# Two selective-scan layers on one core: the instruction order taken from a timeline of engines and queues

## The chip, the cores and the metric

The kernel runs on one core of a Trainium2 chip. Times are device microseconds of one execution. The kernel before takes 29334.67 us, the median of three runs (29313.72 to 29365.72).

A core has five engines that run side by side, each with a queue of its own that is worked off strictly in order: PE (matrix products, written to PSUM), DVE (vector work), ACT (activation functions and copies), POOL (elementwise work in SBUF) and SP (here used to issue DMAs; ACT issues some too). An instruction that depends on another engine waits on a semaphore, and everything queued behind it on its engine waits with it.

## The reference

Sixteen images of 48 x 48 positions with 96 channels go through two layers. Each layer is a state-space block (a "selective scan" in four directions) and a small feed-forward net with values rounded to 8-bit floats. In outline, with the shapes of one image (L = 48 x 48 = 2304):

```python
xc, z = split(layernorm(x) @ in_proj_w.T)            # 192 channels each
xc = silu(depthwise_conv3x3(xc) + conv_b)
xs = [rows, columns, rows reversed, columns reversed]   # 4 directions of xc
dts, B, C = split(x_proj_w @ xs)                     # 6, 16 and 16 rows per direction
delta = softplus(dt_proj_w @ dts + dt_proj_b)
for t in range(L):                                   # 192 channels x 16 states x 4 directions
    h = exp(delta[t] * A) * h + (delta[t] * xs[t]) * B[t]
    y[t] = sum_over_states(h * C[t])
y = merge of the four directions + Ds * xs
# layer 0: y * silu(z) -> out_proj, plus a branch: 1x1, depthwise 3x3 (384 channels), 1x1, gate
# layer 1: layernorm(y) * silu(z) -> out_proj
x = x + that
x = x + feed_forward(layernorm(x))                   # fp8 products, fp16 sums
```

## The kernel before, in words

**The scan.** For each image and layer the recurrence is done by `scan` (line 448). A tile has 128 partitions: 32 channels times 4 states. Along the free axis lie 768 of the 2304 positions. One *step* is one such tile; a layer of one image takes 288 of them (two pairs of directions, three blocks of positions `c`, three blocks of channels `j`, four groups of channels `i`, four groups of states `g`), and the whole kernel 9216. A step does this:

```python
nc.scalar.activation(a, d[:, 0, :], AF.Exp, scale=rates[...])                 # line 484, ACT, into PSUM
nc.gpsimd.tensor_tensor(b, d[:, 1, :], bc[:, 0, :], ALU.mult)                 # line 486, POOL
nc.vector.tensor_tensor_scan(way(h), way(a), way(b), start, ALU.mult, ALU.add)  # line 518, DVE
(nc.vector if here else nc.gpsimd).tensor_tensor(hc, h, cc, ALU.mult)         # line 520
nc.scalar.copy(carry[:, at : at + 1], h[:, last : last + 1])                  # line 522, ACT
nc.tensor.matmul(py[:, q, :SUB], lhsT=self.fold[:, i, :], rhs=hc[...])         # line 524, PE, two of them
```

The scan writes over `a` in three steps of four, and DVE then does the product with C; in the fourth it writes to a tile `h` of its own, and POOL does that product. `a` has two PSUM buffers, `b` four, `hc` four, the loaded `d` (delta and delta times u, line 466) four and `bc` (B and C, line 475) six. The sum over states is left to PE, which adds up 16 steps in the PSUM tile `py`; ACT copies that to `yt` (line 533) and stores it. The first product into `py` (line 504) adds the skip term or the result of the first pair of directions.

**The other work.** Everything that is not a scan runs in Python generators beside the scan of another image or layer: `first` and part of `middle` prepare a scan (`before`, line 346: norm, transposes L300, in-projection L358/L361, convolution L333, SiLU L372, reordered copies L375/L378, the products for B, C and dt L412/L416, `dl` with Softplus L430/L431/L435, `du` on POOL L442, stored by SP L443); `middle` and `final` finish one (`merge` L545 to L553, `gate` L568 to L577, `branch` L593 to L632 with three more convolutions, `centred` L677 to L700, `add_out` L644, `feed_forward` L705 to L742). A 3 x 3 convolution is nine matmuls for each 384 positions (one *chunk*, L333), accumulated in a PSUM tile `pst`. All products of the other work share two buffers of `pst` (line 268), which ACT or DVE empties.

**What sets the order.** `together` (line 781) interleaves one scan of 288 steps, here called a *phase*, with one or two of these generators: after each step it takes as many pieces of the other work as the estimates in the `yield` statements and the totals in `WORK` (line 777) allot to it, up to 94% of the phase (`AHEAD`). There are 32 phases. Two of four hold `final` and `first`, two hold `middle`, which has more convolutions.

This Python order is not yet the order on the engines. The kernel is written in a layer that records instructions and the tiles they touch, and orders them on leaving its context (line 890). Its scheduler plays the program on a model of the machine: an instruction is issued to its engine's queue when, in that model, its inputs are there and its buffers are free, and among those that are ready the one recorded first goes first. The result is one fixed list per engine, with semaphore waits added afterwards. How long things take in the model therefore decides which instruction stands before which on the same engine.

## Time and profile before

| | us |
|---|---|
| median of three runs | 29334.67 |
| the profiled execution | 29326.56 |
| its span, first to last instruction | 29324.8 |
| PE busy | 24033.6 |
| PE weight loads | 12726.8 |
| DVE busy | 23488.3 |
| POOL busy | 23241.6 |
| ACT busy | 14074.7 |
| mean granted PE clock | 0.898 |

The page names a group of instructions by line, engine, operation and tiles (output <- inputs), its shape and count; then its busy time and the mean of one in ns; then the idle time of the engine just before these instructions, and which instruction ended most of it. A fp32 matmul shows as two passes (x36864 for 18432 instructions). In the list of waits a row reads: the engine and instruction that waited, the one that it waited for, microseconds in total, number of waits, the longest. In the timeline a row reads: start, duration, engine, line, operation, tiles, count, and in brackets the idle time before it and what ended it. A row of the stretches gives for each engine the busy time and the number of instructions in that window.

By phase, the profile is very regular: phases with `middle` take about 937 us, the others about 882 us; the first scan starts at 214.6 us, and the last ends about 167 us before the end.

### The profile page before, as it was taken

Reading aid. Unit: us, or ns where it says so; the run is one execution under the profiler, and the core shown is the slowest. Engines: PE = TensorE matmul, PEld = TensorE weight load, DVE = VectorE, ACT = ScalarE, POOL = GpSimd, SP = SyncE. Lnnn points to the kernel's source line nnn. Section 1 sums busy time; section 2 is a strip of 40 time slices with the busy share of each in tenths; the row PEclk is TensorE's granted clock in tenths of the full one; section 3 lists DMA queues with packets and bytes.
Section 4 is the critical chain, followed back from the end, with each engine's and each line's share of the span. In section 5 each row is a group of like instructions: output and inputs, shape, how many; then the busy total and the mean of one; then the engine's idle time right before and its main releaser. Section 6 shows DMA issues by size and latency. Waiting matters only on the chain. (4 is left out here: it accounts for less than half of the span.)

```text
span 29324.8 us, 227106 instructions
## 1 busy us (share of the span) xinstructions
PE 24033.6 (82%) x68224; PEld 12726.8 (43%) x68224; DVE 23488.3 (80%) x18372; ACT 14074.7 (48%) x22093; POOL 23241.6 (79%) x13238
## 2 busy tenths in 40 slices
PE   7888878888788887888788887888778888788886
PEld 3444444444444444444444444444444444344443
DVE  6877888778887788877888778887788877888777
ACT  4454444544445454444444444444444444444443
POOL 6877788778887788877888778787787877877777
PEclk8988899989999899998999989999898998989988
DMA  4444444444444444444444444444444344443443
GB/s 155 153 156 152 146 148 155 154 151 149 148 152 154 154 152 148 148 156 149 159 143 151 151 149 160 144 148 153 150 164 145 141 154 150 162 148 143 150 156 109
DMA packets 1062581, 4406.37 MB, mean 150 GB/s; under 512 B 211936, under 2 KB 211936, under 8 KB 1030368
## 3 DMA queue, kind: packets, MB, share of 16 engines
q1 hardware_dynamic: 869792, 3757.78, 36.2%
q10 hardware_dynamic: 191552, 634.06, 5.5%
q8 instruction: 536, 8.78, 0.1%
q14 instruction: 701, 5.74, 0.1%
HBM read 3500.22 MB, written 891.22 MB: 150 GB/s over the span
## 5 line engine op out<-in xcount | busy, mean ns | idle before, releaser
L486 POOL TENSOR_TENSOR b<-d,bc 128x768 f32<-128x768 f32 x9216 | 16584.7, 1819 | 4084.2 <-DVE a L518 2783.7
L524 PE MATMUL py<-hc,fold_sb 128*128 128x384 f32 x36864 | 14564.0, 540 | 3265.9 <-DVE hc L520 1991.2
L524 PEld LDWEIGHTS py<-hc,fold_sb 128*128 128x128 f32 x36864 | 7359.8, 208 | 9807.3 <-DVE hc L520 3050.8
L484 ACT ACTIVATE a<-d,l_a 128x768 f32<-128x768 f32 x9216 | 8304.2, 906 | 5248.7 <-DVE h L518 2817.0
L518 DVE TENSOR_TENSOR_SCAN a<-a,carry,b 128x768 f32<-128x768 f32 x4608 | 8252.7, 1813 | 2037.9 <-ACT a L484 1438.6
L520 DVE TENSOR_TENSOR hc<-a,bc 128x768 f32<-128x768 f32 x6912 | 6427.8, 947 | 1034.1 <-PE py L524 873.5
L520 POOL TENSOR_TENSOR hc<-h,bc 128x768 f32<-128x768 f32 x2304 | 4187.6, 1818 | 1511.8 <-DVE h L518 1115.4
L518 DVE TENSOR_TENSOR_SCAN a<-a,b 128x768 f32<-128x768 f32 x2304 | 4002.9, 1755 | 1091.6 <-ACT a L484 612.1
L522 ACT COPY carry<-a 128x1 f32<-128x1 f32 x4608 | 725.2, 158 | 5229.7 <-DVE hc L520 5210.7
L518 DVE TENSOR_TENSOR_SCAN h<-a,carry,b 128x768 f32<-128x768 f32 x1536 | 2766.9, 1801 | 484.0 <-ACT a L484 354.4
L333 PE MATMUL pst<-e,dg 128*128 128x384 f32 x5184 | 1730.3, 486 | 0.0
L430 PE MATMUL pst<-dts,wpack_sb 24*128 24x384 f32 x2304 | 1200.8, 636 | 513.9 <-ACT dl L431 434.2
L518 DVE TENSOR_TENSOR_SCAN h<-a,b 128x768 f32<-128x768 f32 x768 | 1337.2, 1741 | 303.9 <-POOL b L486 236.0
L333 PEld LDWEIGHTS pst<-e,dg 128*128 128x128 f32 x5184 | 977.2, 189 | 705.5 <-PE py L524 25.5
L333 PE MATMUL pst<-wxa,dg 128*128 128x384 f32 x3456 | 1173.3, 492 | 24.9 <-DMA dg<-taps_l0a 20.0
L442 POOL TENSOR_TENSOR du<-dl,u 128x768 f32<-128x768 f32 x576 | 1033.6, 1809 | 201.2 <-DMA dd<-du 100.4
L333 PE MATMUL pst<-wxb,dg 128*128 128x384 f32 x3456 | 1169.7, 489 | 5.6 <-issue 5.6
L431 ACT ACTIVATE dl<-pst,wpack_sb 128x384 f32<-128x384 f32 x1152 | 644.0, 577 | 1072.5 <-PE pst L430 581.4
L430 PEld LDWEIGHTS pst<-dts,wpack_sb 24*128 24x128 f32 x2304 | 446.7, 223 | 1206.6 <-ACT dl L431 661.4
L504 PE MATMUL py<-first,ident 128*128 128x384 f32 x1152 | 570.7, 629 | 484.5 <-ACT yt L533 479.6
L412 PE MATMUL pst<-u,wpack_sb 128*24 128x384 f32 (+1 forms) x2304 | 831.7, 492 | 65.2 <-ACT u L395 23.0
L333 PEld LDWEIGHTS pst<-wxa,dg 128*128 128x128 f32 x3456 | 661.5, 192 | 509.4 <-issue 44.6
(143 smaller groups left out, 15283.5 us busy)
## 6 DMA issues: line engine op xcount, KB each, us to landing
d<-dd SPq DMA_DIRECT2D x2304, 768.0 KB, 4.6
bc<-bc SPq DMA_DIRECT2D x1536, 768.0 KB, 6.0
dd<-dl ACTq DMA_DIRECT2D x192, 1152.0 KB, 4.7
dd<-du SPq DMA_DIRECT2D x576, 384.0 KB, 2.5
y<-yt ACTq DMA_DIRECT2D x576, 384.0 KB, 3.1
u<-u ACTq DMA_DIRECT2D x96, 1152.0 KB, 5.1
first<-u SPq DMA_DIRECT2D x288, 384.0 KB, 3.3
first<-y SPq DMA_DIRECT2D x288, 384.0 KB, 3.1
```

What stands on the lines that cost most here:

```text
L333: nc.tensor.matmul(img(o[:, :SUB]), lhsT=dg[:, k, :], rhs=img(p, PW)[:, PQ * q + i : PQ * q + i + PQ, j : j + HW], start=(k == 0), stop=(k ...
L412: nc.tensor.matmul(o[:m, :SUB], lhsT=w[:, j, :], rhs=u[j][:, cs], start=(j == 0), stop=(j == 2))
L430: nc.tensor.matmul(o[:, :SUB], lhsT=dtw[:, col, :], rhs=dts[:, cs], start=True, stop=True)
L431: nc.scalar.activation(dl[:, cs], o[:, :SUB], AF.Identity, bias=self.get(t + "dtb")[:, col : col + 1])
L442: nc.gpsimd.tensor_tensor(du, dl[:, cs], u[j][:, cs], ALU.mult)
L484: nc.scalar.activation(a, d[:, 0, :], AF.Exp, scale=rates[:, pair, j, i, g : g + 1])
L486: nc.gpsimd.tensor_tensor(b, d[:, 1, :], bc[:, 0, :], ALU.mult)
L504: nc.tensor.matmul(py[:, q, :SUB], lhsT=self.skip[t][:, j, :] if pair == 0 else self.ident, rhs=first[:, q * SUB : (q + 1) * SUB], start=True,
L518: nc.vector.tensor_tensor_scan(way(h), way(a), way(b), start, ALU.mult, ALU.add)
L520: (nc.vector if here else nc.gpsimd).tensor_tensor(hc, h, cc, ALU.mult)
L522: nc.scalar.copy(carry[:, at : at + 1], h[:, last : last + 1])
L524: nc.tensor.matmul(py[:, q, :SUB], lhsT=self.fold[:, i, :], rhs=hc[:, q * SUB : (q + 1) * SUB], start=False, stop=((i, g) == (3, GROUPS - 1)),
```

## The change

One argument is given where the context is opened. The scheduler then plays the program against another model of the machine, a timeline of engines and DMA queues, in place of its simpler one. The kernel's functions, tiles, buffer counts and arithmetic stay as they are, and each instruction stays on its engine.

```diff
-    with tile.TileContext(nc) as tc:
+    with tile.TileContext(nc, schedule_with_timeline_sim=True) as tc:
         metaformer_kernel(
```

What this does to the lists: all five engines' orders differ. Laid side by side, with equal neighbours merged into one row, PE has 15334 rows before and 13550 after, DVE 14876 and 14704, ACT 19726 and 19916, POOL 6573 and 6811, SP 3617 and 3823. Scans, exps and `b` products each keep the order of the steps; how the other work stands between them is new.

## The prediction

> **What bounds the kernel now.** First the page's busy part and its groups:
>
> ```profile
> span 29324.8 us, 227106 instructions
> PE 24033.6 (82%) x68224; PEld 12726.8 (43%) x68224; DVE 23488.3 (80%) x18372; ACT 14074.7 (48%) x22093; POOL 23241.6 (79%) x13238
> ...
> L486 POOL TENSOR_TENSOR b<-d,bc 128x768 f32<-128x768 f32 x9216 | 16584.7, 1819 | 4084.2 <-DVE a L518 2783.7
> L524 PE MATMUL py<-hc,fold_sb 128*128 128x384 f32 x36864 | 14564.0, 540 | 3265.9 <-DVE hc L520 1991.2
> ...
> L518 DVE TENSOR_TENSOR_SCAN a<-a,carry,b 128x768 f32<-128x768 f32 x4608 | 8252.7, 1813 | 2037.9 <-ACT a L484 1438.6
> L520 DVE TENSOR_TENSOR hc<-a,bc 128x768 f32<-128x768 f32 x6912 | 6427.8, 947 | 1034.1 <-PE py L524 873.5
> ```
>
> Three engines stand at 80% and none at 100%: the bound changes from stage to stage. The work is 9216 scan steps. A step is exp on ACT (L484), `b` on POOL (L486), scan on DVE (L518), product with C (`hc`, L520, on DVE in three steps of four, on POOL in the fourth) and two fold matmuls on PE (L524). Four steps cost DVE 4 x 1.81 + 3 x 0.95 = 10.1 us. DVE is idle for 29324.8 - 23488.3 = 5836 us, and that is all that a new order could win.
>
> Next, who makes DVE wait (the list of waits, DVE alone), and two stretches of one middle phase by engine:
>
> ```profile
> DVE a L518 <- ACT a L484: 2050.8, 1411, 13.0
> DVE a L518 <- ACT carry L522: 905.8, 859, 11.3
> DVE hc L520 <- PE py L524: 873.5, 695, 5.7
> DVE h L518 <- ACT a L484: 361.9, 171, 6.5
> ```
>
> ```profile
> core 0: us, PE busy (x) PEld busy (x) DVE busy (x) ACT busy (x) POOL busy (x), PEclk, DMA share, GB/s
> 8499.00:8538.00 39.00, 39.00 (x122) 22.71 (x121) 33.26 (x28) 16.82 (x31) 26.87 (x16) 1.00 0.46 166
> 9131.00:9182.00 51.00, 40.40 (x84) 17.99 (x84) 29.42 (x22) 29.16 (x36) 40.69 (x23) 0.80 0.64 236
> ```
>
> Both stretches hold 12 steps, which DVE could do in 30 us. In the first (convolution) PE never rests; in the second (softplus) ACT's long instructions hold up the exps, and 12 steps take 51 us. The timeline shows the convolution case:
>
> ```profile
> 8511.95 5.97 PE L333 MATMUL pst<-e,dg 128*128 128x384 f32 x18
> ...
> 8519.04 5.32 PE L524 MATMUL py<-hc,fold_sb 128*128 128x384 f32 x16
> ...
> 8521.83 0.96 DVE L520 TENSOR_TENSOR hc<-a,bc 128x768 f32<-128x768 f32 x1 [2.44 <-PE py L524]
> ```
>
> One convolution chunk (nine products, 18 passes) is 5.97 us, four steps' folds are 5.32 us: together 11.3 us against DVE's 10.1. With one chunk per four steps PE is just the bound, and DVE waits for a free `hc` buffer (four of them).
>
> **What a page says.** The Trainium skill, Perfetto Trace Analysis, Optimization Strategy: where the most-contended engine changes over time, interleaving those regimes can help. The trace agrees that there are regimes (PE 39.00 us of 39.00 in one, ACT 29.16 us in the other, against 16.82). So I ask of the new order whether it mixes these regimes more or less; the forecast goes by counted durations, not by the page.
>
> **The change.** No operation is added or removed but five activation-table loads (825 become 830, 1.28 us each by this trace, +6 us) and some 650 separate semaphore waits (30,592 become 31,240, some 20 ns each, spread over five engines: nothing). Each engine's instructions are issued in another order, which the two programs' orders show. Scan, exp and `b` stay in step order; what moves is everything between them. I give every instruction of both orders the step that it stands behind on its own engine, and the duration that it has in the trace of before (0.645 us for a 384-column matmul of two passes).
>
> *PE.* Between two steps' folds, the old order has never more than one convolution chunk and odd pieces: no gap over 10 us. The new one has 98 such gaps, 94 of them two chunks or more in a row (one 24 us), most near steps 190 to 225 of a 288-step phase, where the in-projection's convolution lies. In stretches of 12 steps, those with over 40 us of PE work go from 2 to 56; PE work above 37 us, summed, from 133 to 918 us. To price this I take in each of the 768 stretches the busiest engine's work and sum: 26,931 us before (the measured scan part is 28,945), 27,434 after: +503. With stretches of 24 steps, which lets the four `hc` buffers smooth more, 26,511 becomes 26,808: +297. Both ends are kept; I take **+400**.
>
> *ACT.* A foreign instruction between two exps costs DVE nothing until the two `a` buffers are used up. Foreign ACT work by four steps against DVE's idle time in them, in the trace: 1.1 us idle with under 1 us of it, 3.8 at 5, 7.5 at 8, 17 at 17. That table, with the new order's counts, gives 5489 before and 5433 after: -56. By stretches of 12 steps the new order looks better: those with over 25 us on ACT fall from 144 to 100, and with the excess over the busiest engine that such stretches show before (14 us where ACT has 31 to 35 us; 62 of these become 19), -697. But part of those now lies beside PE lumps, and single gaps over 3.5 us between exps sum the same (1051 and 1059 us). I take **-150**.
>
> *PE and PSUM.* PE's results are read by ACT some 2 to 3 steps later in the order than before (dt matmuls to `dl`: 3.7 steps become 6.8; h1 copies 2.4 become 4.6). This spares ACT some waiting at the head of its queue; walking back from each DVE stall, such waits cover 490 us of the 5836. But PSUM has two `pst` buffers, and the matmul that takes a buffer stands by as much further ahead of the reader that frees it: for the in-projection's convolutions it stood 2 steps behind that reader and now stands 3 to 4 ahead. PE waits there, and folds are queued behind. While DVE has free `hc` buffers this costs nothing; at five steps ahead they are full, and exp 0.9 + eviction 0.6 + chunk 6.0 + fold 1.3 = 8.8 us stand against 5 us of DVE work: 3.8 us each. A quarter to a half of 256 such chunks give 240 to 490 us, less the 490 above at best, and most lie in the stretches already priced. I take **+100**, ends -490 and +490.
>
> *DVE.* Its pattern by four steps becomes regular: scan, scan, scan, product, product, scan, product in 838 of 2304 groups (293 before). At best this leaves 0.47 us idle in the trace, the old common ones 0.36 to 0.38: 545 x 0.1 = **+50**.
>
> *POOL, SP and ACT's queue.* The fourth step's `hc` stands 4.3 instead of 3.5 `b`s late on POOL, within four `b` and four `hc` buffers; POOL's own lumps shrink a little (work above 31 us per stretch 1368 to 1215; in the sums). SP's stores of `du` stand behind loads of `d` 11 steps ahead instead of 7; a `d` load can go out about 12 steps ahead, so they still fit, barely. The `bc` loads hardly move (3.4 to 3.1 steps ahead), so POOL's 815.6 us of waiting for them stays. I take 0, ends -100 and +200.
>
> The 214 us before the first scan and the 164 us after the last stay: nothing overlaps them. **Sum:** 400 - 150 + 100 + 50 + 6 = +406 us. On the profiled execution's 29326.6 us that is 29,733; on the median of the runs, 8 us higher, 29,741. I say 29,740 (+1.4%).
>
> **Rivals.**
> 1. *Faster:* the coarse ACT count is the true one and the `hc` buffers soak up the PE lumps: -697 + 297 + 6 = -394, 28,940 us. For it: ACT waits (2051 + 362 + 906 us) are DVE's largest. Against: the sum of single lumps is unchanged, and DVE has two `a` buffers, not twelve. It decides where softplus and silu stretches shrink by more than 400 us in all.
> 2. *Much slower:* waits for `pst` come at full price: 503 + 490 + 50 = +1043, 30,380 us. For it: an order fixed for each queue turns every mistimed wait into a stall of all that is behind it. Against: DVE can still run four steps ahead of PE.
> 3. *No change:* what is won at ACT is lost at PE, 29,335 us. That needs a coincidence.
> That the change does not do what it says is excluded: every engine's order differs.
>
> **How the numbers follow.** Likeliest case 0.53, own range 29,450 to 30,050; rival 1 0.23; rival 2 0.18; rival 3 0.06. The range 28,900 to 30,500 reaches into both outer cases and leaves about one in ten out at each end. A measurement of this kernel tells about 0.2% from no change (its three runs lie within 0.18%). So faster 0.23, same 0.06, slower 0.71.
>
> **What would show it.** Right: PE's waits stay or grow while DVE's wait for `py` (873.5 us) about doubles; stretches with 35 to 60 us of PE work per 12 steps in the second half of a phase, DVE idle there; DVE's wait for exp (2050.8) a little lower; PE waiting at L333 for ACT (L361, L367, L387), absent now. Busy sums unchanged within 1%. Wrong: DVE's wait for `py` unchanged, or the softplus stretches down from 51 us to 40. A change over 4% either way would mean a mechanism that I have not seen, most likely SP's or POOL's order.

## The result, and the profile after

The changed kernel takes 29435.97 us (median of 8 runs, 29424.53 to 29466.74) against 29339.03 us for the kernel before (8 runs): 1.0032 times as long, 95% interval 1.0022 to 1.0043. It is slower, as forecast, but by 97 us (0.3%) and not by 406. That is nearer to the third rival of the prediction (no change, 29,335 us) than to its forecast (29,740). Costs and gains of several hundred microseconds nearly cancel; one of them I had priced with the wrong sign, and one stood in no step of my sum.

The page of the changed kernel, busy part and the groups that answer to those shown before:

```profile
span 29441.0 us, 227759 instructions
PE 24141.4 (82%) x68224; PEld 13110.4 (45%) x68224; DVE 23695.4 (80%) x18372; ACT 14116.6 (48%) x22098; POOL 23179.6 (79%) x13238
...
L524 PE MATMUL py<-hc,fold_sb 128*128 128x384 f32 x36864 | 14261.8, 541 | 1909.2 <-POOL hc L520 1285.1
...
L518 DVE TENSOR_TENSOR_SCAN a<-a,carry,b 128x768 f32<-128x768 f32 x4608 | 8258.9, 1811 | 1043.9 <-ACT a L484 690.2
...
L520 DVE TENSOR_TENSOR hc<-a,bc 128x768 f32<-128x768 f32 x6912 | 6495.0, 951 | 2692.4 <-PE py L524 2397.4
```

Durations are as they were (a scan 1811 ns, a product 951, a fold pass 541). What changed is the last column. Idle time in front of this scan went from 2037.9 to 1043.9 us, idle time in front of the product from 1034.1 to 2692.4. DVE's list of waits in the changed kernel says for whom:

```profile
DVE hc L520 <- PE py L524: 2397.4, 1304, 28.7
DVE a L518 <- ACT a L484: 1065.6, 782, 11.7
DVE a L518 <- ACT carry L522: 555.0, 708, 10.8
...
DVE h L518 <- ACT a L484: 170.4, 70, 11.4
```

The waits for ACT (exp and carry, both scans) sum to 3447 us before and 1911 after, 1536 us less. The wait for PE to free an `hc` went from 873.5 to 2397.4 us, 1524 us more. DVE's idle time as a whole went from 5836 to 5746 us (span less busy), while its busy time rose from 23488.3 to 23695.4: +207 - 91 = +116 us, the difference of the two spans.

Where PE holds up DVE is seen in the timeline of the changed kernel, in the in-projection's convolution of a middle phase:

```profile
8963.58 11.78 PE L333 MATMUL pst<-wxa,dg 128*128 128x384 f32 x36
...
8975.19 1.45 PE L524 MATMUL py<-hc,fold_sb 128*128 128x384 f32 x4
...
8976.48 11.78 PE L333 MATMUL pst<-wxa,dg 128*128 128x384 f32 x36
8976.73 1.81 POOL L520 TENSOR_TENSOR hc<-h,bc 128x768 f32<-128x768 f32 x1 [8.46 <-PE py L524]
8982.49 0.58 ACT L367 ACTIVATE u<-pst,wpack_sb 128x384 f32<-128x384 f32 x1 [6.51 <-PE pst L333]
...
8988.09 1.45 PE L524 MATMUL py<-hc,fold_sb 128*128 128x384 f32 x4
...
8989.58 0.96 DVE L520 TENSOR_TENSOR hc<-a,bc 128x768 f32<-128x768 f32 x1 [25.65 <-PE py L524]
```

Two chunks in a row (11.78 us), one step's four passes (1.45 us), two chunks again, and all four `hc` are full. The buffer that the passes between the two pairs free goes to POOL's product, so DVE stands for 25.65 us, until the passes behind the second pair free another. The stretches of the same phase by engine, 11 or 12 scans in each row (scans 197 to 207 and 208 to 218 of the phase, and the softplus part, 245 to 256 and 257 to 268):

```profile
core 0: us, PE busy (x) PEld busy (x) DVE busy (x) ACT busy (x) POOL busy (x), PEclk, DMA share, GB/s
8959.00:9032.00 73.00, 66.51 (x194) 37.73 (x193) 27.32 (x19) 31.14 (x40) 31.29 (x21) 0.93 0.21 72
9032.00:9079.00 47.00, 47.00 (x145) 26.03 (x144) 28.60 (x21) 26.60 (x40) 25.16 (x14) 1.00 0.42 159
9146.00:9179.00 33.00, 27.17 (x65) 14.04 (x64) 29.10 (x22) 17.02 (x18) 32.45 (x20) 0.81 0.49 174
9179.00:9214.00 35.00, 30.47 (x72) 15.14 (x72) 28.63 (x22) 18.72 (x22) 28.20 (x16) 0.83 0.63 229
```

The first row has 66.51 us of PE work against 27.32 of DVE's. The last two take 33 and 35 us; before, the softplus stretch shown in the prediction (scans 256 to 267 of this phase) took 51. Averaged over phases 4 to 27, the time of 24 steps from the times of the scans in the two traces:

```
from step                  0    24    48    72    96   120   144   168   192   216   240   264   sum
phases with middle
  before                83.2  61.2  76.2  74.3  78.1  80.6  81.9  69.3  87.8  82.3  94.1  68.4  937.4
  after                 77.8  81.4  69.4  66.4  68.2  78.7  79.8  75.5  98.0 100.6  66.5  68.7  931.0
phases with final, first
  before                72.4  89.0  60.5  70.6  75.3  68.2  80.8  69.2  72.4  79.8  76.3  66.5  881.0
  after                 74.5  81.0  87.1  79.4  74.1  68.2  84.3  67.3  66.1  68.0  71.0  72.0  893.0
```

The middle phases gain 24.6 us in steps 48 to 119 (the branch's convolutions) and 27.6 in steps 240 to 263 (softplus), and lose 28.5 in steps 192 to 239 and 20.2 in steps 24 to 47. Softplus and `du` are no longer packed into the end of a phase: 122 of the 192 Softplus stood in steps 240 to 263 before, 50 do now, and the first 48 steps of a phase hold about 55 instead of 5 or 6. Of the 576 `du`, 338 stood in those 24 steps, and 143 do now.

The sums tell one thing more. The middle phases as a whole gain 6 us each; it is the phases with `final` and `first` that lose, 12 us each. Their largest loss is in steps 48 to 95 (35.5 us), where products that finish a scan (L568, L688, L644) now stand close together: in steps 48 to 71 PE's work goes from 51.7 to 75.9 us, without one convolution, and DVE's idle time from 1.0 to 21.0.

### The profile page after: what moved, and what is told of

Its sections match the earlier page's. It is cut to its first block, busy times and chain, and to the rows that moved or that the text cites. A ratio compares the mean times of both kernels' runs of the same rounds, so it can differ in the third digit from the quotient of the medians.

```text
span 29441.0 us, 227759 instructions
## 1 busy us (share of the span) xinstructions
PE 24141.4 (82%) x68224; PEld 13110.4 (45%) x68224; DVE 23695.4 (80%) x18372; ACT 14116.6 (48%) x22098; POOL 23179.6 (79%) x13238
## 5 line engine op out<-in xcount | busy, mean ns | idle before, releaser
L524 PE MATMUL py<-hc,fold_sb 128*128 128x384 f32 x36864 | 14261.8, 541 | 1909.2 <-POOL hc L520 1285.1
L524 PEld LDWEIGHTS py<-hc,fold_sb 128*128 128x128 f32 x36864 | 7670.9, 213 | 8284.2 <-issue 1839.3
L518 DVE TENSOR_TENSOR_SCAN a<-a,carry,b 128x768 f32<-128x768 f32 x4608 | 8258.9, 1811 | 1043.9 <-ACT a L484 690.2
L520 DVE TENSOR_TENSOR hc<-a,bc 128x768 f32<-128x768 f32 x6912 | 6495.0, 951 | 2692.4 <-PE py L524 2397.4
L333 PE MATMUL pst<-e,dg 128*128 128x384 f32 x5184 | 1723.5, 486 | 0.0
L430 PE MATMUL pst<-dts,wpack_sb 24*128 24x384 f32 x2304 | 1119.6, 605 | 448.4 <-ACT dl L431 440.0
L333 PEld LDWEIGHTS pst<-e,dg 128*128 128x128 f32 x5184 | 980.5, 189 | 701.5 <-PE py L524 36.2
L333 PE MATMUL pst<-wxa,dg 128*128 128x384 f32 x3456 | 1142.2, 486 | 17.1 <-DMA dg<-taps_l0a 15.3
L333 PE MATMUL pst<-wxb,dg 128*128 128x384 f32 x3456 | 1145.2, 486 | 4.1 <-ACT wxb L361 4.1
L504 PE MATMUL py<-first,l_skip 128*128 128x384 f32 x1152 | 576.9, 635 | 386.7 <-ACT yt L533 375.9
L333 PEld LDWEIGHTS pst<-wxa,dg 128*128 128x128 f32 x3456 | 654.8, 190 | 482.8 <-issue 22.3
```

The lines of the kernel that those rows point to most:

```text
L333: nc.tensor.matmul(img(o[:, :SUB]), lhsT=dg[:, k, :], rhs=img(p, PW)[:, PQ * q + i : PQ * q + i + PQ, j : j + HW], start=(k == 0), stop=(k ...
L430: nc.tensor.matmul(o[:, :SUB], lhsT=dtw[:, col, :], rhs=dts[:, cs], start=True, stop=True)
L504: nc.tensor.matmul(py[:, q, :SUB], lhsT=self.skip[t][:, j, :] if pair == 0 else self.ident, rhs=first[:, q * SUB : (q + 1) * SUB], start=True,
```

## The experiments

To hold an order while something else is changed, a kernel was built twice. The first build asks one of the two schedulers for its lists; the second adds edges between neighbours on an engine, which fix the order and add no wait:

```diff
+    traced = list(nc.cur_bb.bb.instructions)
+    for line in pinned:
+        for before, after in zip(line, line[1:]):
+            tc.add_manual_dep(traced[after], traced[before].name,
+                mybir.DependencyInfo(mybir.DependencyClass.NoSync, mybir.DependencyReason.DATA),
+                reason="pinned")
```

With all five engines held, work can be cut or buffers added in the second build, and each list stays that of the kernel before ("old") or of the changed kernel ("new"). The traces bear this out: in all eight such builds PE, DVE, ACT and POOL run their instructions in exactly the order of the kernel whose lists they hold. Where a cut removes nothing, the time stays too: in the lists of before, steps 0 to 95 of a middle phase take the same in act_cut_old and du_fill_old to 0.1 us per 24 steps. A difference of two cuts is uncertain by some 70 us (the intervals of the ratios, added in quadrature).

### PE's order alone

```diff
-    with tile.TileContext(nc) as tc:
+    with tile.TileContext(nc, schedule_with_timeline_sim=timeline) as tc:
+FROM, TIMELINE, PINNED = False, True, (mybir.EngineType.PE, )   # pe_old; pe_new: True, False
```

In pe_old the timeline schedules everything, but PE keeps the old list. In pe_new the old scheduler runs, and PE is held to the new list.

> The timeline schedules everything, but PE is held to the order that it has in the kernel before. Theory 1 (the two changes add up: 1500 us won at exp, 1500 us lost at the folds): DVE's wait for py goes back to 0.9 ms, its waits for exp and carry stay near 1.9 ms, time near 28,000 us. Theory 2 (displacement: while DVE stands at a fold, ACT catches up, so that the same lateness is only booked elsewhere): waits for exp and carry rise again to 3 ms or more, time within 1% of 29,340.

> The simple scheduler orders everything, but PE is held to the order that the timeline gave it. Theory 1: the fold waits of 2.4 ms come on top of the old exp waits of 3.4 ms, time near 30,800 us. Theory 2: the exp waits shrink to about 2 ms all the same, since DVE stands at folds instead; time 29,300 to 29,800.

Measured: pe_old 30523.81 us, 1.0405 of before (1.0390 to 1.0421); pe_new 29941.34, 1.0208 (1.0191 to 1.0225). Each mixture is slower than both kernels. The waits of DVE in pe_old:

```profile
DVE hc L520 <- PE py L524: 2934.3, 1577, 16.4
DVE a L518 <- ACT a L484: 1471.0, 1119, 10.6
```

PE's list is that of the kernel before and has next to none of the lumps (two stretches of 12 steps with over 40 us of PE work, against 56 in the changed kernel), and yet DVE waits longer for `py` than in any other run. PE itself stands at instructions whose producers now come later: 1309 us for `dl` (L431), 778 for `xm` (L289). So a list is good or bad only against the other four. Neither theory held: pe_old lies far above the times of both, pe_new between them. The share of PE can't be read off from these two runs, and the next ones hold all five lists.

### Two more hc buffers, all five lists held

```diff
-            hc = self.sw.tile([128, CH], F32, name="hc", bufs=4)
+            hc = self.sw.tile([128, CH], F32, name="hc", bufs=6)
```

> Every engine keeps exactly the order of the changed kernel; hc has six buffers instead of four, so DVE may run two steps further ahead of the folds. Theory 1: most gaps of PE over 10 us are covered, DVE's wait for py falls from 2.4 to about 1.2 ms and the time by about 1 ms, to 28,400. Theory 2: py waits fall, waits for exp rise by as much, time above 29,100.

> Every engine keeps exactly the order of the kernel before; hc has six buffers. Both theories: DVE's wait for py is 0.87 ms and most of it lies where PE has no rest at all (convolution stretches), which buffers can't mend; gain of 100 to 500 us, time 28,850 to 29,250. If it gains as much as the same buffers in the new order, then the new order's fold waits are no special weakness.

Measured: hc6_new 29200.73 us, 0.9954 of before (0.9939 to 0.9969), 235 us less than the changed kernel; hc6_old 29134.34, 0.9932 (0.9917 to 0.9947), 198 us less than before. The two gains differ by less than their uncertainty. The waits of DVE in hc6_new:

```profile
DVE a L518 <- ACT a L484: 1649.4, 954, 26.1
DVE a L518 <- ACT carry L522: 1084.2, 1094, 25.6
DVE hc L520 <- PE py L524: 511.9, 238, 14.9
```

The wait for `py` fell by 1886 us, from 2397.4 to 511.9, and the time by an eighth of that. DVE's waits for exp and carry took up 1425 us. The longest single ones grew to 26 us: stalls as long as that of 25.65 us are still there, under another label. A reading of this is that ACT's list is as fixed as PE's, and with more `hc` free DVE runs ahead until it stands for ACT. A row of the list of waits is therefore not the price of its cause. The page Perfetto Trace Analysis of the Trainium skill says, in its section Optimization Strategy, that gaps which repeat over a stretch can mean too few buffers for the next tile. The trace has such gaps, and buffers remove the label, but most of the time comes back under the next one.

### Shorter convolutions

Eight of the nine taps of each chunk cover one row of eight. The count of instructions stays, and the convolutions' passes take 1818 instead of 4073 us in the old lists, 55% less (the sums of their groups). Left out are these eight taps for seven rows of eight.

```diff
+                n = 1 if CUT and k else PQ
-                    img(o[:, :SUB]),
+                    img(o[:, :SUB])[:, :n], lhsT=dg[:, k, :],
-                    rhs=img(p, PW)[:, PQ * q + i : PQ * q + i + PQ, j : j + HW],
+                    rhs=img(p, PW)[:, PQ * q + i : PQ * q + i + n, j : j + HW],
```

> Every engine's order is that of the kernel before; in each convolution chunk taps 2 to 9 cover one image row of eight (work left out), which should take about 3.5 us off each of 672 chunks. Only the stretches where PE has no rest should gain: DVE's wait for py, 0.87 ms, falls to 0.3 ms or less, time about 28,700 us.

> The same cut in the order of the changed kernel. Theory A (two chunks in a row are what the new order loses by): DVE's wait for py falls from 2.4 ms to under 1 ms without its waits for exp rising, and the time falls under that of the old order with the same cut, to about 28,000 us. Theory B (the fold waits come from where PE's and ACT's instructions stand against each other, PE waiting for a PSUM buffer that ACT frees late, whatever the chunk costs): py wait stays above 1.5 ms or turns into waits for exp, and the time stays at or above that of the old order with the cut.

Measured: conv_cut_old 28752.47 us, 0.9801 (0.9787 to 0.9816); conv_cut_new 28564.87, 0.9734 (0.9718 to 0.9750). The cut is worth 586 us in the old lists and 871 in the new: the part of the convolutions that is cut costs the new order 285 us more, and without it the new order is the faster one, by 188 us. By 24 steps of a middle phase, steps 192 to 239 fall by 28.5 us with the new lists (98.0 + 100.6 to 85.1 + 85.0) and do not fall with the old; steps 48 to 119 fall by 24.4 with the old and 9.3 with the new. The new order treats the branch's convolutions better and the in-projection's worse. With the cut, the new order's loss in steps 192 to 239 is gone (170.1 against 170.5); over 16 such phases that is, by my estimate from these averages, some 460 us, against which some 240 of its gain in the branch go too. In the phases with `final` and `first` the cut changes little: the new order's loss there goes from 12 to 11 us. The wait for `py` (list of waits, conv_cut_new) is still well above that of before, so theory A holds for the time but not for this wait:

```profile
DVE hc L520 <- PE py L524: 1539.2, 928, 18.0
DVE a L518 <- ACT a L484: 1086.2, 845, 11.9
```

### Shorter ACT instructions

Softplus and SiLU take a sixth of their elements, and the three reordering copies run straight. The other elements of these activations and the copies' reordering are left out; `dl` goes through Relu, which keeps the exps bounded.

```diff
-                nc.scalar.activation(dl, dl, AF.Softplus)
+                nc.scalar.activation(part(dl), part(dl), AF.Softplus)
...
-                nc.scalar.copy(swapped(u[1][64:]), img(u[0][64:]))
+                nc.scalar.copy(way(u[1][64:]), img(u[0][64:]))
...
```

> Every engine's order is that of the kernel before; Softplus and SiLU cover a sixth of their elements, the three reordering copies copy in straight order, and dl is clipped at zero (work left out and changed). Some 700 us less on ACT in long instructions. Where long instructions of ACT are what the old order loses by, it gains at least that: DVE's waits for exp and carry fall from 3.4 to about 2.4 ms, time 28,300 to 28,500 us.

> The same cut in the order of the changed kernel. If the new order already hides these instructions, as its shorter waits for exp (1.9 ms) suggest, it gains half of what the old order gains or less, time about 29,000 us. If the waits for exp are only displaced to the folds (py 2.4 ms), the cut gains as much as in the old order, time about 28,500.

Measured: act_cut_old 29013.18 us, 0.9889 (0.9874 to 0.9904), a gain of 326 where I expected more than 800; act_cut_new 28849.66, 0.9830 (0.9815 to 0.9845), a gain of 586 over the changed kernel. A Softplus now takes 523 ns instead of 2126, and yet the old lists' softplus stretch (steps 240 to 263 of middle phases) goes only from 94.1 to 91.3 us. The length of Softplus is not most of what makes that stretch slow: 8.0 us less of it on ACT give 2.8. Its activation-table loads, 1.28 us before each Softplus and most often 1.28 again before the next exp, are untouched by the cut, so their price is not measured. The same skill page says, in Optimizing Scalar/DVE Operations, that breaking up instructions on an unsaturated ACT or DVE may help where they cause gaps elsewhere. No run here breaks one up; the run that shortens Softplus gains 3 us of some 34 lost in that stretch (94.1 against 60 for DVE's own work).

The sign is also the opposite of what I believed: what is cut of the long instructions costs the *new* order 260 us more (586 - 326). The difference is not bound to the lumps: steps 192 to 239 of middle phases fall by 9.8 us in the new lists and 9.4 in the old. It is spread over the stretches into which Softplus has moved: steps 0 to 47 fall by 4.4 us in the new lists and by nothing in the old, steps 264 to 287 fall by 1.8 and rise by 2.3. A reading of this is that a Softplus costs its length where ACT stands for nothing else, and is covered where ACT would have stood for `dl` anyway; no run separates that.

### POOL's du without dl

If the length isn't it, what is? The timeline of the kernel before, in the softplus stretch:

```profile
9132.64 1.05 ACT L431 ACTIVATE dl<-pst,wpack_sb 128x384 f32<-128x384 f32 x2 [4.34 <-POOL du L442]
...
9136.47 0.90 ACT L484 ACTIVATE a<-d,l_a 128x768 f32<-128x768 f32 x1
...
9137.47 1.82 DVE L518 TENSOR_TENSOR_SCAN h<-a,carry,b 128x768 f32<-128x768 f32 x1 [4.96 <-ACT a L484]
...
9153.65 1.05 ACT L431 ACTIVATE dl<-pst,wpack_sb 128x384 f32<-128x384 f32 x2 [4.96 <-POOL du L442]
...
9154.60 0.91 ACT L484 ACTIVATE a<-d,l_a 128x768 f32<-128x768 f32 x1
...
9155.60 1.82 DVE L518 TENSOR_TENSOR_SCAN h<-a,carry,b 128x768 f32<-128x768 f32 x1 [3.93 <-ACT a L484]
```

`dl` (a cheap 0.58 us copy) stands at the head of ACT's queue for 4 to 5 us, until POOL has read the last `dl` for `du` and its buffer is free. The exp queued behind it has to wait too, and DVE then waits for the exp. ACT's own list of waits shows the same, first before, then after:

```profile
ACT dl L431 <- PE pst L430: 581.4, 357, 6.4
...
ACT dl L431 <- POOL du L442: 476.0, 127, 8.5
...
ACT u L367 <- PE pst L333: 146.8, 34, 28.1
```

```profile
ACT u L367 <- PE pst L333: 596.5, 132, 22.6
...
ACT dl L431 <- PE pst L430: 133.9, 160, 5.3
...
ACT dl L431 <- POOL du L442: 22.3, 14, 7.7
```

Between the first and the last scan, ACT stood idle with an instruction of the other work (none of exp, carry, `yt`) at the head of its queue for 3905 us before and 1985 after. By whom it waited for, PE's part fell from 3064 to 1771 us and POOL's from 577 to 59. To test POOL's part, POOL fills `du` with a constant (the product of delta and u is left out), so that `dl`'s buffer comes free without POOL. POOL's busy time falls by 620 us in both orders (a `du` takes 0.74 us instead of 1.81), so only the difference between them speaks of the order.

```diff
-                    nc.gpsimd.tensor_tensor(du, dl[:, cs], u[j][:, cs], ALU.mult)
+                    nc.gpsimd.memset(du, 0.01) if CUT else nc.gpsimd.tensor_tensor(du, dl[:, cs], u[j][:, cs], ALU.mult)
```

> Every engine's order is that of the kernel before; POOL fills du with a constant instead of multiplying (work left out), which takes up to 1 ms off POOL and frees dl without waiting for POOL. In the old order ACT stands 0.48 ms with a dl copy (L431) at the head of its queue until POOL has read an earlier dl, with exps behind it. If that queue position is what makes the softplus stretch slow in the old order (94 us per 24 steps in middle phases, 66.5 in the new), the wait goes, the stretch falls under 80 us and the time by 500 us or more, to 28,800. If long ACT instructions are to blame, it gains little: above 29,150.

> The same fill in the order of the changed kernel, where that wait is 0.02 ms. If the new order gains because it no longer has a dl copy ahead of its buffer, it has little left to win here: under 300 us, time 29,150 or more, above the old order with the same fill. If both gain alike, POOL's load and not the position was the price.

Measured: du_fill_old 28887.89 us, 0.9841 (0.9825 to 0.9858), 455 us less than before, the softplus stretch down from 94.1 to 77.6 us; du_fill_new 29384.43, 1.0017 (1.0009 to 1.0024), 52 us less than the changed kernel, the stretch 66.5 and 66.3. So the old order loses 403 us more than the new one by POOL's `du` and what waits for it, and the new order next to nothing.

Whether it is the place of `dl` or the load of POOL is not separated. POOL's total falls alike in both orders, but not where it counts. In the softplus stretch of the old lists 13.3 `du` stand per phase, and POOL is busy for 80 of the 94.1 us (55 of work for the scan, as in other stretches, and 24 of `du`); the fill takes 14.5 us off POOL there. In the new lists 3.3 `du` stand there, and it takes off 3.5. During the 476 us for which ACT's `dl` waited for `du`, POOL was at work for 400 (on `du` 284). For the place speaks that ACT's wait for `du` in that stretch, 15.6 us, vanishes and that its idle time falls by 16.5, just as the stretch does. Both come from the same packing of `dl`, Softplus and `du` at the end of a phase, which the timeline has spread out. A run that frees `dl` and leaves POOL's load as it is would tell them apart; none was made.

### Six hc buffers, lists free

> The kernel before with six hc buffers, ordered anew by the simple scheduler. As with six buffers in the fixed old order (29,134 us), 29,050 to 29,250.

> The changed kernel with six hc buffers, ordered anew on the timeline. With the fixed new order six buffers gave 29,201 us; the timeline now puts 4410 products right behind their own scan (2867 with four buffers). If two or three scans in a row matter to DVE, this costs: 29,250 to 29,450; if not, 29,000 to 29,250.

The edit of the buffers again, but each scheduler may now make its lists anew for six. Measured: hc6_free_old 28841.02 us, 0.9829 (0.9814 to 0.9844), and hc6_free_new 29174.05, 0.9943 (0.9928 to 0.9958). The first beats both kernels, by 502 us against before, and lies some 200 us under the range that I had expected. It is 293 us below the same buffers with the old lists held, though the buffers are the same: the scheduler uses them. DVE's list of waits in hc6_free_old:

```profile
DVE a L518 <- ACT a L484: 1889.5, 1267, 13.1
DVE a L518 <- ACT carry L522: 571.5, 715, 10.7
...
DVE hc L520 <- PE py L524: 448.4, 453, 6.5
```

The wait for `py` halves against before, and this time the wait for the carry does not rise in exchange (for both scans 845 us, against 1035 before and 1392 in hc6_old). With the timeline the gain of free lists over held ones is small (29174 against 29201).

## Why the prediction was right in direction and wrong in size

The three pairs of cuts can be set beside the prediction's own terms, new order against old:

| step of the prediction | taken | measured by |
|---|---|---|
| *PE*, chunks in a row | +400 (297 to 503) | conv_cut pair: +285 (cut of 55%) |
| *ACT*, long foreign instructions | -150 (-697 to -56) | act_cut pair: +260 (lengths cut, table loads left) |
| *PE and PSUM*, ACT's waits for PE, PE's for `pst` | +100 (-490 to +490) | no run |
| *DVE*, pattern | +50 | no run |
| ACT's `dl` behind POOL's `du` | in no step | du_fill pair: -403 |
| sum (with 6 for table loads) | +406 | the three pairs +142; the kernels themselves +97 |

Each pair is uncertain by some 70 us, each cut removes only a part, the parts overlap, and two steps have no run. That +142 lies near +97 is therefore no proof that the account is complete. It is not: the loss of 35 us in steps 48 to 95 of the phases with `final` and `first` stands at 34 to 38 in all four held pairs, and so does most of the middle phases' 20 us in steps 24 to 47 (18.5 to 20.7). Gains elsewhere offset these, and no cut prices either.

**Where it failed: the ACT step, and a wait that no step has.** I priced ACT's foreign work by its length, from a table of foreign work by four steps against DVE's idle time. That table was a correlation: the stretches with much foreign work on ACT are those where `dl`, Softplus and POOL's `du` stand packed. Cutting Softplus to a quarter of its time moved that stretch by 3 us of 94, and over the kernel the lengths speak against the new order, by 260 us, where I had taken 150 for it. What the new order does win there, 403 us, hangs on POOL's `du`. The prediction's row for that stretch has POOL at 40.69 us of 51 and PE at 40.40, both above ACT's 29.16, and yet I read it as ACT's; ACT's wait for `du` (476.0 us) is in none of my steps, for the 490 us that I walked back to belong to PE's results.

The PE-and-PSUM step stays open. ACT's waits for PE at the head of its queue fell by 1293 us, and no run takes them away by themselves. The price that I expected for `pst` did not appear as a wait: PE's idle time ahead of the convolutions (L333) sums to 21 us in the changed kernel, 4.1 of it for ACT (groups by line). In the lumps shown it is DVE and ACT that stand for PE, not the other way round.

**Right.** The *PE* step: lumps of two chunks near steps 190 to 225 of a phase, with DVE waiting; the cut gives +285, just under the low end of its range, and as it removes only 55% of the chunks' time, the whole may be more. The wait for `py` did rise, to 2.7 times instead of double. Busy sums stayed within 1% (DVE +0.9%), PE's weight loads apart (+3.0%).

**Right by luck.** The sign of the sum. It came out as forecast because terms of the size of the forecast itself nearly cancel; with the convolutions cut, the new order is the faster one. This is close to the third rival, "what is won at ACT is lost at PE", which I gave 0.06. The one thing named as proof against the forecast, a softplus stretch falling from 51 us to 40, came true (33 and 35), and with it half of the *faster* rival: its gain in those stretches was there (27.6 us in each middle phase), and other stretches took it back, the lumps with the most. The "little lower" wait for exp was 1536 us lower, with the carry's.

**Not forecast.** The *DVE* step took +50 us for the pattern. DVE's busy time rose by 207 us, which was in no step. By the trace, instructions that overlap their predecessor overlap 100 us less in all, and 108 us lie in longer durations (the largest part `hq` casts of the feed-forward, L722 and L724, and the products themselves). No run tested this by itself, so how much of it reached the end stays open. That the scheduler's own idea of durations causes the lumps was not tried either; the runs show what the two orders cost, not why the timeline chose its own.

## What to carry to other kernels

Judge a new order on in-order queues by what stands at the head of each queue without its inputs or its buffer while a critical instruction is behind it; here a short copy that waited for another engine's packed work went with a loss of some 400 us, while shortening the long activations in the same stretch gained little there. Look at every engine's load in such a stretch, not only at the one that the critical engine waits for. A row in the list of waits is a label and not a price: when one resource is enlarged, check which label takes over, and cut the suspected work with the order held in order to price it. And let the scheduler reorder after buffers change: six `hc` buffers gave 198 us with the old lists held and 502 with new ones (with the timeline the two differ little, 235 and 262).

## What the hardware showed that I had not expected

A product that stands directly behind the scan whose output it reads does not overlap with it at all in these traces (0 ns, 1535 cases before and 2867 after, of 6912 products); behind another step's scan the overlap was 79 ns on average before and 61 after. With more such pairs the overlap of all products with their predecessor fell from 404 to 235 us, that of the scans rose by 78. The regular pattern of the *DVE* step thus costs busy time on DVE, where I had looked for idle time.

The mean granted PE clock does not rank these kernels: 0.898 before, 0.874 after, 0.847 in conv_cut_new, which takes the least time of all (with work left out). A fold pass takes 540, 541 and 550 ns in these three.
